# Sums of the experts' results in parts: quarters for one chunk behind the first mixture, halves for the last two chunks

## Chip, cores and metric

The kernel runs on one core of a Trainium2 chip. The metric is the device time of one execution in microseconds (us); a profile is one more execution of the same program.

## The reference

Two layers work on 4096 tokens of 256 numbers in float32, with a 4096 x 4096 adjacency matrix. Each layer is a graph step followed by a mixture of experts, both with a layer norm ahead and a residual around:

```
x = x + gnn0(layernorm(x), adj)          # graph step, then a state-space scan
x = x + moe0(layernorm(x))               # 8 experts, the best 2 for each token
x = x + gnn1(layernorm(x), adj, adj)     # tanh(adj*adj), 700 largest of each row kept
x = x + moe1(layernorm(x))               # 6 experts, the best 2 for each token
```

A mixture's output for a token is `w0 * y0 + w1 * y1`: the outputs of its two experts with the routing weights. In the second graph step the node features are `h = tanh(xn @ W_proj + b)`, then `g = h @ W_gcn`, and the result is `relu(A @ g + b)` with A the filtered adjacency matrix.

## The kernel before

Tokens go in chunks of CW = 512, of TPC = 4 tiles of 128 tokens; there are NC = 8 chunks. Token data lies with 128 tokens on the partitions.

**A mixture** first routes all tokens, then runs tiles of 256 gathered tokens (`expert_tiles`): SyncE (SP) loads the experts' weights `wk` and `bk`, POOL gathers the tokens `xk` with indirect DMAs, TensorE (PE) multiplies (`ps_xt`, `ps_h`, `ps_y`), and VectorE (DVE) adds the bias into `yk`. `put` (L391) then scatters `yk` by indirect DMA into a DRAM tensor `ys`, where every token has one row for its first and one for its second expert, arranged so that the four rows of a partition lie together: 4 KB for one partition of a chunk. The DMAs that scatter are kept in `dp.sent`.

**`combine`** fetches these rows again and sums. For each of the two experts it loads one tile `yg` (L516, 128 x 4 x 256, 512 KB; the pool has three such buffers) with an order behind the last four scatters, then makes eight `scalar_tensor_tensor` operations on VectorE (L524): for each of the four tiles of tokens, first `src + w0*yg0`, then `+ w1*yg1`. After the first mixture source and destination are both `x2`. After the second, the source is `x3`, the destination a tile `oc` that `to_out` stores to `out` (L1470).

**Between the first mixture and the second graph step**, `features_of` calls `combine` and then `node_features` for one chunk after each two pieces of the graph step's first column block: `layernorm` of the four tiles (statistics L76 and L77, the addition of eps L78 on VectorE, the power -0.5 on POOL L79, then `xn` on VectorE L81), TensorE transposes (L91, all four token tiles of column block 0, then all four of block 1), ACT copies them to `xnT` (L1359), TensorE makes `ps_lt` with `w_proj` (L140), ACT the tanh, TensorE `ps_gn` (L1367), ACT copies `gn`.

**The graph step** `propagate1(c)` goes through sixteen pieces of 256 rows of the transposed adjacency matrix: SP loads `at` (L1381, 512 KB, four buffers), VectorE makes `f = max(at, 0)` (L1387), ACT squares it and takes the tanh, VectorE counts the positive entries into `cnt` (L1392 for the first piece of a column block, L1394 for the others), and TensorE adds `gn x f` into `pf` (L1398). For column block 0, two pieces are done per chunk of features. So TensorE's order there is, for each chunk, transposes, `ps_lt`, `ps_gn`, then `pf` for two pieces.

**At the end**, the second mixture is in two dispatches: tokens of the first six chunks (`dp1[0]`), and of the last two (`dp1[1]`). The first six chunks' outputs are summed and stored while the second dispatch's tiles run. The last two chunks (`for b in range(NC - SPLIT)`) come when all its tiles are done. Behind the whole stands a test (`flag`) for a rarely needed second way, which begins with a full top-700 selection and then repeats the mixture; it is not taken with these inputs.

**What sets the order**: the middle of the program (the scan) has an order written out by hand. Around the change no order is written: a scheduler of the framework orders each engine's instructions when the program is built, and the engines then take them strictly in that order. SP issues its DMAs in order as well, so a DMA that waits for a buffer holds up those behind it.

Of the kernel before, what the change touches and what calls it, by code (L numbers as in the profile page):

```python
# [9 lines left out]
F32 = mybir.dt.float32  # L10
# [3 lines left out]
ALU = mybir.AluOpType  # L14
# [4 lines left out]
P = 128  # L19
CW = 512  # L20
TPC = CW // P
# [7 lines left out]
def kernel(ctx: ExitStack, tc: tile.TileContext, out: bass.AP, **a):  # L29
    nc = tc.nc  # L30
    x, adj, adjT = a["x"], a["adj"], a["adjT"]
    N, D = x.shape
# [12 lines left out]
    def tokens(ap, c):  # L45
        return ap[c * CW:(c + 1) * CW, :].rearrange("(t p) d -> p t d", p=P)
# [22 lines left out]
    def layernorm(src, dst):  # L69

        T = src.shape[1]
        st = small.tile([P, T, 6], F32, name="ln_st")
        mv = small.tile([P, T, 2], F32, name="ln_mv")
        rs = small.tile([P, T], F32, name="ln_rs")
        for t in range(T):
            nc.vector.bn_stats(st[:, t, :], src[:, t, :])  # L76
            nc.vector.bn_aggr(mv[:, t, :], st[:, t, :])  # L77
        nc.vector.tensor_scalar(rs, mv[:, :, 1], EPS, None, ALU.add)  # L78
        nc.gpsimd.tensor_tensor(rs, rs, mhalf[:, :T], ALU.pow)  # L79
        for t in range(T):  # L80
            nc.vector.tensor_scalar(  # L81
                dst[:, t, :], src[:, t, :], mv[:, t, 0:1], rs[:, t:t + 1],
                ALU.subtract, ALU.mult,
            )
# [60 lines left out]
    def after(later, earlier):  # L145
        tc.add_manual_dep(
            later.ins, earlier.ins.name,
            mybir.DependencyInfo(mybir.DependencyClass.Sync, mybir.DependencyReason.DATA),
            reason="order",
        )  # L150
# [355 lines left out]
                also(n)  # L506
        finish(*prev)

    def combine(dp, pool, c, src, dst):


        yg = []
        for i in range(2):
            yg.append(pool.tile([P, TPC, D], F32, name="yg", bufs=3))
            r0 = (i * dp.S + c) * CW
            ld = nc.sync.dma_start(  # L516
                yg[i], dp.ys[r0:r0 + CW, :].rearrange("(p t) d -> p t d", t=TPC)
            )
            for o in dp.sent[-4:]:
                after(ld, o)  # L520
        for t in range(TPC):
            s_ = c * TPC + t
            for i in range(2):
                nc.vector.scalar_tensor_tensor(  # L524
                    dst[:, t, :], yg[i][:, t, :], dp.wv[:, s_, i:i + 1], (src, dst)[i][:, t, :],
                    ALU.mult, ALU.add,
                )

    r0 = ctx.enter_context(tc.tile_pool(name="route0", bufs=1))
# [7 lines left out]
    with ExitStack() as s1:  # L539
# [44 lines left out]
        dp = Dispatch(r0, E0, "d0", [NT - 2 * TPC, 2 * TPC])  # L584
# [571 lines left out]
        with tc.manual_schedule(engines={  # L1156
# [11 lines left out]
            for _ in range(2 * NT + 2):  # L1168
                i = min(range(STEPS), key=lambda i: pe[i] - PE_RATIO * dve[i])
# [23 lines left out]
            for n in range(NC * STEPS):  # L1193
                c, i = divmod(n, STEPS)
# [24 lines left out]
                old, das = das, []  # L1219
# [52 lines left out]
    x2 = keep.tile([P, NT, D], F32, name="x2")  # L1272
    wp = ctx.enter_context(tc.tile_pool(name="w_ffn0", bufs=1, reuse_waits="tile"))
    with ExitStack() as s2:
        with ExitStack() as st:
# [47 lines left out]
        x3 = keep1.tile([P, NT, D], F32, name="x3")  # L1323
# [9 lines left out]
        dp1 = [  # L1333
            Dispatch(keep1, E1, "d1a", [TPC] * SPLIT),
            Dispatch(keep1, E1, "d1b", [TPC] * (NC - SPLIT), SPLIT),
        ]
# [15 lines left out]
        ps_f = s2.enter_context(tc.tile_pool(name="ps_f", bufs=2, space=PSUM, reuse_waits="tile"))  # L1352
        ps_m = s2.enter_context(tc.tile_pool(name="ps_m1", bufs=4, space=PSUM, reuse_waits="tile"))

        def node_features(c):
            xn = wk.tile([P, TPC, D], F32, name="xn", tag="xn_r")
            layernorm(x2[:, c * TPC:(c + 1) * TPC, :], xn)
            xT = wk.tile([P, DB, CW], F32, name="xnT2", tag="fm", bufs=4)
            transpose_chunk(ps_m, "m", xn, lambda k, ps: nc.scalar.copy(xT[:, k, :], ps))  # L1359
            h2 = wk.tile([P, DB, CW], F32, name="h2", tag="fm", bufs=4)  # L1360
            layer_T(ps_m, "m", xT, w_proj, AF.Tanh, b_proj, h2, DB, DB)
            for hh in range(TPC // 2):
                ps = ps_m.tile([P, 2, D], F32, name="ps_gn", tag="m")
                for j in range(2):
                    t = 2 * hh + j
                    for k in range(DB):
                        nc.tensor.matmul(  # L1367
                            ps[:, j, :], h2[:, k, t * P:(t + 1) * P], w_gcn[:, k, :],
                            start=(k == 0), stop=(k == DB - 1),
                        )  # L1370
                t0 = c * TPC + 2 * hh
                nc.scalar.copy(gn[:, t0:t0 + 2, :], ps)
# [47 lines left out]
        def features_of(j2):  # L1420

            if j2 % (TPC // 2) == 0:
                c = j2 // (TPC // 2)
                rows = x2[:, c * TPC:(c + 1) * TPC, :]
                combine(dp, wk, c, rows, rows)
                node_features(c)

        early = [route1(d, wk, ps_m, ("m", "m", "m"), 4) for d in dp1]

# [32 lines left out]

    stores = []

    def to_out(d, b, pool):

        c = d.c0 + b
        o = pool.tile([P, TPC, D], F32, name="oc")
        combine(d, pool, b, x3[:, c * TPC:(c + 1) * TPC, :], o)
        return nc.sync.dma_start(tokens(out, c), o)  # L1470


    few = [2 * d.NT * P // TR + E1 // 2 for d in dp1]
    with ExitStack() as s4:
        tp = s4.enter_context(tc.tile_pool(name="tiles1", bufs=2, reuse_waits="tile"))
        psums = [
            s4.enter_context(tc.tile_pool(name=n, bufs=f, space=PSUM, reuse_waits="tile"))
            for n, f in (("ps_h1", 3), ("ps_o1", 2), ("ps_t1", 2))
        ]
        ps_r = s4.enter_context(tc.tile_pool(name="ps_r1", bufs=1, space=PSUM, reuse_waits="tile"))  # L1480
        sr = ExitStack()
        rp = sr.enter_context(tc.tile_pool(name="route1", bufs=2, reuse_waits="tile"))
        late = route1(dp1[1], rp, ps_r, ("m", "m", "m"), 1)

        def routing():
            late.prepare(NC - 1 - SPLIT)
            yield
            late.choose(NC - 1 - SPLIT)
            yield
            yield from dp1[1].tables(  # L1490
                ps_r.tile([P, CW], F32, name="ps_inv", tag="m"), rp, [eb1, eb2]
            )

        pieces = routing()
        ready, op = list(range(SPLIT)), []

        def also(n):
            if n == few[0]:
                assert next(pieces, None) is None
                sr.close()  # L1500
                op.append(s4.enter_context(tc.tile_pool(name="out1", bufs=2, reuse_waits="tile")))
            elif n < few[0]:
                if n > 0:
                    next(pieces, None)
            elif (n - few[0]) % 3 != 0 and ready:
                stores.append(to_out(dp1[0], ready.pop(0), op[0]))

        tiles1([(d, k) for d, f in zip(dp1, few) for k in range(f)], psums, tp, also)
        assert not ready

        for b in range(NC - SPLIT):
            stores.append(to_out(dp1[1], b, op[0]))


        flag = small.tile([1, 1], F32, name="flag", bufs=1)
        flagi = small.tile([1, 1], I32, name="flagi", bufs=1)
        nc.vector.tensor_reduce(flag, cmax, AX.X, ALU.max)
        nc.vector.tensor_scalar(flag, flag, TOPK + 0.5, None, ALU.is_gt)
        for d, f in zip(dp1, few):
            nc.vector.scalar_tensor_tensor(flag, d.tiles, f + 0.5, flag, ALU.is_gt, ALU.add)  # L1520

        after(nc.vector.tensor_copy(flagi, flag), dp1[1].sent[-1])
        again = nc.values_load(flagi[0:1, 0:1], min_val=0, max_val=3)
# [3 lines left out]
    with tc.If(again > 0):  # L1527
# [57 lines left out]
        with ExitStack() as s3:  # L1585
            kp = s3.enter_context(tc.tile_pool(name="again", bufs=1))
            d = Dispatch(kp, E1, "d2", [TPC] * NC)
            d.lo = lo1
            with ExitStack() as sr:
                ps_r = sr.enter_context(tc.tile_pool(name="ps_r2", bufs=2, space=PSUM))  # L1590
                rp = sr.enter_context(tc.tile_pool(name="route2", bufs=1))
                rt = route1(d, rp, ps_r, ("m", "m", "m"), 1)
                for c in range(NC):
                    rt.prepare(c)
                    rt.choose(c)
                for _ in d.tables(ps_r.tile([P, CW], F32, name="ps_inv", tag="m"), rp, [eb1, eb2]):
                    pass
            psums = [
                s3.enter_context(tc.tile_pool(name=n, bufs=f, space=PSUM))
                for n, f in (("ps_h2", 3), ("ps_o2", 2), ("ps_t2", 2))  # L1600
            ]
            with tc.tile_pool(name="tiles2", bufs=2) as tp:
                tiles1([(d, k) for k in range(d.K)], psums, tp)
            op = s3.enter_context(tc.tile_pool(name="out2", bufs=1))
            for c in range(NC):
                after(to_out(d, c, op), stores[c])


# [65 lines left out]
```

## Time and profile before

| | |
|---|---|
| median of 3 runs | 2479.3 us (2477.19 to 2481.99) |
| the profiled execution's own time | 2478.58 us |
| its span, first to last instruction | 2476.7 us |
| mean granted TensorE clock | 0.956 of full speed |
| busy share of the span: PE, DVE, ACT, POOL | 91%, 67%, 48%, 46% |
| sums `x<-yg` behind the first mixture | 64, from 1633.2 to 1697.6 us |
| sums `oc<-yg` of the last two chunks | 16, from 2462.5 to 2469.7 us |
| loads `yg<-d_ys` of 512 KB | 16, median 4.4 us from issue to landing |

Times in the views are microseconds from the start of the span; a line of a timeline gives start, duration, engine, line of the kernel, operation and tiles, and in brackets the idle time of the engine before it with what ended it. SPq is SP's queue: it issues DMAs and the duration is that of the issue, not of the transfer. In the chain of waits each piece is the step that ended last, followed back from the end.

### The profile page before, as it was taken

What the parts mean: (1) busy time and instruction counts of PE and PEld (TensorE: products, weight loads), DVE (VectorE), ACT (ScalarE), POOL (GpSimd) and SP (SyncE); (2) the same over time, 40 slices, a digit from 0 to 9 for tenths busy, and PEclk for the clock granted to TensorE, in tenths of its full rate; (3) what the DMA queues carried; (4) which work ended last, traced back from release to release, by engine and by line L of the source; (5) the groups of instructions that cost most, each with busy time, mean ns of one, the idle gap of its engine ahead of it and who ended that gap; (6) DMA issues with size and microseconds to landing.
All of it is one profiled execution on the core that took longest, in us unless ns stands there. A gap on an engine that the chain in (4) does not pass through costs nothing. (4 is left out here: it accounts for less than half of the span.)

```text
span 2476.7 us, 25809 instructions
## 1 busy us (share of the span) xinstructions
PE 2259.5 (91%) x8024; PEld 1448.7 (58%) x8024; DVE 1652.7 (67%) x2368; ACT 1194.0 (48%) x2029; POOL 1141.4 (46%) x830
## 2 busy tenths in 40 slices
PE   5989989999999999896994999969999999989985
PEld 4765655646565565643663888845544444458874
DVE  4049999999999999989897111165466666744233
ACT  1135657465665657466662322224566566633321
POOL 1027677777767677776551455411000000026652
PEclk9989999999999999997996999989999999999998
DMA  6259898999999999988655777743344444447886
GB/s 205 94 161 240 229 269 225 268 220 269 238 244 266 234 264 231 274 239 216 214 175 172 232 232 233 216 162 108 102 145 146 144 146 149 139 133 235 245 279 233
DMA packets 290500, 509.33 MB, mean 206 GB/s; under 512 B 25376, under 2 KB 157600, under 8 KB 289456
## 3 DMA queue, kind: packets, MB, share of 16 engines
q1 hardware_dynamic: 244080, 410.55, 52.9%
q0 software_dynamic: 46272, 97.03, 18.3%
q8 instruction: 67, 1.10, 0.2%
q14 instruction: 81, 0.66, 0.1%
HBM read 406.03 MB, written 42.73 MB: 181 GB/s over the span
## 5 line engine op out<-in xcount | busy, mean ns | idle before, releaser
L1103 POOL TENSOR_TENSOR db<-du,bb 128x1024 f32<-128x1024 f32 x256 | 607.0, 2371 | 359.5 <-ACT state L1124 132.4
L1118 DVE TENSOR_TENSOR_SCAN db<-da,state,db 128x512 f32<-128x512 f32 x512 | 627.5, 1267 | 45.7 <-ACT da L1111 43.4
L642 PE MATMUL pt<-at,gn 128*128 128x256 f32 x2048 | 488.2, 391 | 33.9 <-DVE ln_mv L77 27.4
L1111 ACT ACTIVATE da<-dt,negA 128x512 f32<-128x512 f32 x512 | 347.5, 691 | 354.3 <-DVE db L1118 352.5
L642 PEld LDWEIGHTS pt<-at,gn 128*128 128x128 f32 x2048 | 398.3, 196 | 164.7 <-issue 74.6
L1398 PE MATMUL pf<-f,gn 128*128 128x512 f32 x1024 | 450.4, 594 | 0.0
L1145 PE MATMUL psy<-hc,ident 128*128 128x512 f32 x576 | 304.3, 622 | 46.5 <-DMA hc<-hc 40.1
L1128 DVE TENSOR_TENSOR hc<-db,cb 128x1024 f32<-128x1024 f32 x256 | 331.8, 1296 | 17.9
L1398 PEld LDWEIGHTS pf<-f,gn 128*128 128x128 f32 x1024 | 191.5, 190 | 224.9 <-issue 223.8
L79 POOL TENSOR_TENSOR ln_rs<-ln_rs,mhalf 128x4 f32<-128x4 f32 x24 | 34.5, 1436 | 513.4 <-DVE ln_rs L78 454.0
L460 DVE TENSOR_TENSOR yk<-ps_y,bk 128x512 f32<-128x512 f32 x73 | 50.5, 691 | 326.9 <-PE ps_y L455 302.4
L470 PE MATMUL ps_h<-xkT,wk 128*128 128x256 f32 x864 | 214.7, 390 | 12.5 <-DVE xkT L495 8.4
L1388 ACT ACTIVATE f<-f 128x1024 f32<-128x1024 f32 x128 | 135.3, 1057 | 180.6 <-DVE f L1387 178.8
L455 PE MATMUL ps_y<-wk,hk 128*128 128x256 f32 x864 | 210.9, 380 | 0.2
L1387 DVE TENSOR_SCALAR f<-at 128x1024 f32<-128x1024 f32 x128 | 88.2, 689 | 174.9 <-PE pf L1398 158.1
L1132 POOL DMA_DIRECT2D hc<-hc x224 | 195.0, 870 | 0.2
L470 PEld LDWEIGHTS ps_h<-xkT,wk 128*128 128x128 f32 x864 | 160.7, 194 | 47.1 <-ACT hk L474 11.2
L1145 PEld LDWEIGHTS psy<-hc,ident 128*128 128x128 f32 x576 | 110.5, 198 | 122.9 <-issue 51.2
L455 PEld LDWEIGHTS ps_y<-wk,hk 128*128 128x128 f32 x864 | 161.4, 190 | 21.8 <-ACT hk L474 1.3
L474 ACT ACTIVATE hk<-ps_h,d_b 128x256 f32<-128x256 f32 x140 | 66.2, 474 | 184.2 <-PE ps_h L470 184.2
L1394 DVE SCALAR_TENSOR_TENSOR cnt<-at,cnt 128x1024 bf16<-128x1024 f32 x120 | 146.1, 1217 | 11.6 <-DMA at<-in_adjT_dram 10.5
L754 PE MATMUL ps_xz<-hT,w_in 128*128 128x512 f32 x256 | 126.4, 630 | 14.7 <-ACT hT L742 14.7
(307 smaller groups left out, 2585.6 us busy)
## 6 DMA issues: line engine op xcount, KB each, us to landing
at<-in_adjT_dram SPq DMA_DIRECT2D x256, 512.0 KB, 4.3
bb<-bcd SPq DMA_DIRECT2D x128, 512.0 KB, 5.1
cb<-bcd SPq DMA_DIRECT2D x128, 512.0 KB, 4.7
hc<-hc POOLq DMA_DIRECT2D x224, 256.0 KB, 5.6
wk<-in_L_ffn_W_dram SPq DMA_DIRECT2D x70, 512.0 KB, 5.0
wk<-in_L_ffn_expert_w_dram SPq DMA_DIRECT2D x114, 256.0 KB, 4.4
yg<-d_ys SPq DMA_DIRECT2D x16, 512.0 KB, 4.4
yd<-us SPq DMA_DIRECT2D x6, 1024.0 KB, 7.9
```

Of the source, the lines that this page charges most:

```text
L455: nc.tensor.matmul(ps[:, j, :], hT[:, m, j * P:(j + 1) * P], w[:, m, :], start=(m == 0), stop=(m == kb_out - 1),)
L470: nc.tensor.matmul(ps[:, j, :], w[:, d, m * P:(m + 1) * P], xT[:, d, :], start=(d == 0), stop=(d == DB - 1),)
L642: nc.tensor.matmul(pt[:, k, :], xl[:, j, k * P:(k + 1) * P], at[:, jj, :], start=(j == 0 and k == 0), stop=(j == NT - 1 and k == DB - 1),)
L1103: nc.gpsimd.tensor_tensor(self.db, self.f.du[self.half][:, self.mi:self.mi + 1, :].to_broadcast([P, 2, CW]), self.bb, ALU.mult,)
L1111: nc.scalar.activation(da, self.f.dt[self.half][:, self.mi, :], AF.Exp, scale=negA[:, self.m, n:n + 1])
L1118: nc.vector.tensor_tensor_scan(self.db[:, j, :], da, self.db[:, j, :], state[:, self.m, n:n + 1], ALU.mult, ALU.add,)
L1128: nc.vector.tensor_tensor(self.hc, self.db, self.cb, ALU.mult)
L1132: nc.gpsimd.dma_start(self.hc[:, 0, :], self.hc[:, 1, :], accum_op=ALU.add)
L1145: nc.tensor.matmul(f.psy[m], ident, self.hc[:, j, :], start=False, stop=(self.g == GS - 1 and j == last),)
L1388: nc.scalar.activation(f, f, AF.Square)
L1394: nc.vector.scalar_tensor_tensor(cnt, at, 0.0, cnt, ALU.is_gt, ALU.add)
L1398: nc.tensor.matmul(pf[:, k, :], gn[:, j, k * P:(k + 1) * P], f[:, jj, :], start=(j == 0), stop=(j == NT - 1),)
```

## The change

`combine` gets a number of parts and becomes a generator: for each part it loads the two `yg` tiles of that part alone (128 x T x 256 with T = 4, 2 or 1), makes the part's sums, and yields. `node_features` now calls `combine` itself and normalises each part as it comes: four parts of 128 tokens for chunk 0, one part for the other seven. `to_out` stores each part by itself: two parts for the last two chunks, one for the first six. The number of `yg` buffers stays three. The loop of the second way at the bottom follows the new return value.

```diff
-    def combine(dp, pool, c, src, dst):
-        yg = []
-        for i in range(2):
-            yg.append(pool.tile([P, TPC, D], F32, name="yg", bufs=3))
-            r0 = (i * dp.S + c) * CW
-            ld = nc.sync.dma_start(
-                yg[i], dp.ys[r0:r0 + CW, :].rearrange("(p t) d -> p t d", t=TPC)
-            )
-            for o in dp.sent[-4:]:
-                after(ld, o)
-        for t in range(TPC):
-            s_ = c * TPC + t
+    def combine(dp, pool, c, src, dst, parts=1):
+        T = TPC // parts
+        for t0 in range(0, TPC, T):
+            yg = []
             for i in range(2):
-                nc.vector.scalar_tensor_tensor(
-                    dst[:, t, :], yg[i][:, t, :], dp.wv[:, s_, i:i + 1], (src, dst)[i][:, t, :],
-                    ALU.mult, ALU.add,
-                )
+                yg.append(pool.tile([P, T, D], F32, name="yg", tag="yg", bufs=3))
+                r0 = (i * dp.S + c) * CW
+                rows = dp.ys[r0:r0 + CW, :].rearrange("(p t) d -> p t d", t=TPC)
+                ld = nc.sync.dma_start(yg[i], rows[:, t0:t0 + T, :])
+                for o in dp.sent[-4:]:
+                    after(ld, o)
+            for t in range(T):
+                s_ = c * TPC + t0 + t
+                for i in range(2):
+                    nc.vector.scalar_tensor_tensor(
+                        dst[:, t0 + t, :], yg[i][:, t, :], dp.wv[:, s_, i:i + 1],
+                        (src, dst)[i][:, t0 + t, :], ALU.mult, ALU.add,
+                    )
+            yield
...
-        def node_features(c):
+        def node_features(c, parts):
+            rows = x2[:, c * TPC:(c + 1) * TPC, :]
             xn = wk.tile([P, TPC, D], F32, name="xn", tag="xn_r")
-            layernorm(x2[:, c * TPC:(c + 1) * TPC, :], xn)
+            T = TPC // parts
+            for i, _ in enumerate(combine(dp, wk, c, rows, rows, parts)):
+                layernorm(rows[:, i * T:(i + 1) * T, :], xn[:, i * T:(i + 1) * T, :])
...
                 c = j2 // (TPC // 2)
-                rows = x2[:, c * TPC:(c + 1) * TPC, :]
-                combine(dp, wk, c, rows, rows)
-                node_features(c)
+                node_features(c, TPC if c == 0 else 1)
...
-    def to_out(d, b, pool):
-        c = d.c0 + b
+    def to_out(d, b, pool, parts=1):
+        c, T = d.c0 + b, TPC // parts
         o = pool.tile([P, TPC, D], F32, name="oc")
-        combine(d, pool, b, x3[:, c * TPC:(c + 1) * TPC, :], o)
-        return nc.sync.dma_start(tokens(out, c), o)
+        sent = []
+        for i, _ in enumerate(combine(d, pool, b, x3[:, c * TPC:(c + 1) * TPC, :], o, parts)):
+            part = slice(i * T, (i + 1) * T)
+            sent.append(nc.sync.dma_start(tokens(out, c)[:, part, :], o[:, part, :]))
+        return sent
...
-            stores.append(to_out(dp1[1], b, op[0]))
+            stores.append(to_out(dp1[1], b, op[0], 2))
...
-                after(to_out(d, c, op), stores[c])
+                for new in to_out(d, c, op):
+                    for old in stores[c]:
+                        after(new, old)
```

## The prediction

> **What bounds the kernel now.** I read the page's line of busy times (PE 91% of the span), then the two places the change touches. The first is the passage from the first mixture to the graph layer. Windows (window: length, then per engine busy time and count, granted PE clock, DMA share, GB/s):
>
> ```profile
> 1621.20:1640.70 19.50, 0.00 (x0) 0.00 (x0) 12.04 (x33) 0.00 (x0) 3.40 (x7) 0.62 0.63 211
> 1640.70:1658.60 17.90, 17.82 (x48) 9.68 (x49) 16.10 (x49) 4.47 (x7) 3.08 (x2) 0.84 0.49 183
> 1658.60:1767.10 108.50, 105.77 (x339) 58.82 (x337) 50.56 (x127) 54.61 (x72) 8.05 (x5) 1.00 0.28 92
> ```
>
> TensorE stands still for 19.5 us, then works without a hole for eight chunks of about 15.3 us. So only what brings its restart at 1640.7 forward or back counts. The chain of waits and the timelines (start, length, what) show what it waits for:
>
> ```profile
> 1605.26 22.73 DMA d_ys<-yk,d_dst
> ...
> 1633.16 3.25 DVE x L524 x8
> ...
> 1638.94 1.22 POOL ln_rs L79
> 1640.18 1.38 DVE xn L81 x4
> ```
>
> ```profile
> 1628.16 1.28 SPq L516 DMA_DIRECT2D yg<-d_ys  x3
> 1628.78 0.69 DVE L1392 TENSOR_SCALAR cnt<-at 128x1024 bf16<-128x1024 f32 x1
> 1629.50 3.74 DVE L1394 SCALAR_TENSOR_TENSOR cnt<-at,cnt 128x1024 bf16<-128x1024 f32 x3
> 1633.16 3.25 DVE L524 SCALAR_TENSOR_TENSOR x<-yg,d_wv,x 128x256 f32<-128x256 f32 x8
> 1640.18 1.38 DVE L81 TENSOR_SCALAR xn<-x,ln_mv,ln_rs 128x256 f32<-128x256 f32 x4 [0.94 <-POOL ln_rs L79]
> 1640.74 2.10 PE L91 MATMUL ps_tr<-ident,xn 128*128 128x128 f32 x8 [19.56 <-DVE xn L81]
> ```
>
> The scattered results land, SP issues the loads at 1628.16, and they land at 1631.7 and 1633.0. VectorE meanwhile does four counts (`cnt`) until 1633.2: **the loads are hidden behind the counts**. From the first sum to the last `xn` (1641.56) are 8.40 us. The second place is the end, where the chain alternates between loads and sums:
>
> ```profile
> 2456.42 2.41 DMA d1b_ys<-yk,d1b_dst
> 2458.98 3.45 DMA yg<-d1b_ys
> 2462.46 1.68 DVE oc L524 x4
> 2464.16 4.25 DMA yg<-d1b_ys
> ```
>
> **The change at the first chunk.** Bytes and sums stay. Two loads of 512 KB become eight of 128 KB, one 128x4 power on POOL becomes four of 128x1, one `ln_rs` addition becomes four. The four counts still stand ahead of the first sum, so quicker first loads gain nothing: the first sum stays at 1633.16. What the diff does not tell is the order of VectorE's instructions in the built program. Three more counts, which in the kernel before come after chunk 1, now stand inside chunk 0:
>
> ```
> sum p0, sum p0, stats p0, sum p1, aggr p0, eps p0, xn p0 [waits POOL],
> CNT, sum p1, sum p2, stats p1, sum p2, aggr p1, stats p2, eps p1,
> CNT, xn p1 [POOL], aggr p2, CNT, eps p2, sum p3, xn p2 [POOL],
> sum p3, stats p3, sum chunk 1, aggr p3, sum chunk 1, eps p3, sum chunk 1, xn p3 [POOL]
> ```
>
> VectorE takes them in order, and transposes, ACT and TensorE stand in the same order as before. TensorE transposes column block 0 of all four parts before block 1, so it goes no further than p3 lets it.
>
> Paces from the timeline, start to start: independent sums 0.40, dependent ones 0.51 (0.48 and 0.03 wait), stats 0.33, aggregate or eps 0.08, `xn` 0.32, a count 1.14 (1.22 less overlap). The power of 128x1 does not occur. Nearest rows:
>
> ```profile
> 1306.75 0.70 POOL L1046 TENSOR_TENSOR x_dev<-x_dev,mhalf 128x2 f32<-128x2 f32 x1 [18.50 <-DVE x_dev L1045]
> 1646.06 1.17 POOL L79 TENSOR_TENSOR ln_rs<-ln_rs,mhalf 128x4 f32<-128x4 f32 x1 [5.92 <-DVE ln_rs L78]
> 1653.89 1.91 POOL L79 TENSOR_TENSOR ln_rs<-ln_rs,mhalf 128x4 f32<-128x4 f32 x1 [6.65 <-DVE ln_rs L78]
> ```
>
> From 128x2 to 128x4 is 0.47, so 128x1 may be 0.55 at best and 1.2 at worst; I take 0.85, nearer to the 128x2 row. The third row ran beside a count and took 0.7 more; of the new powers only p1's does, so it costs 0 to 0.7 (I take 0.35).
> - p0 to the issue of its `xn`: two dependent sums 1.03; stats, sum, aggregate, eps 1.08; POOL 0.97 with its two hand-overs; `xn` 0.32. Sum 3.40.
> - then up to the second count: count 1.14, sums and p1's and p2's statistics 2.04. Sum 3.18.
> - second count 1.14, `xn` 0.32, aggregate 0.09, third count 1.14, eps and hand-over 0.25. Sum 2.94.
> - p2's POOL and hand-over 0.89, `xn` 0.32, last sum 0.51, p3's statistics with two sums of chunk 1 1.45, POOL 0.88, last `xn` 0.41. Sum 4.46.
>
> 13.98 instead of 8.40: **+5.6, with p1's crowded power +5.9**. With powers of 0.55 and none crowded it is +4.7, with 1.2 and 0.7 crowded +7.4. Three counts (3.4) and the three extra trips to POOL make it up.
>
> *Loads.* Three `yg` buffers serve four parts, so a load waits for the sum that frees a buffer: p1's second load goes at 1633.7, p2's at 1634.2 and 1635.0, p3's at 1638.2 and 1638.6. A lone 128 KB load (`rw`) landed in 2.1, a 512 KB one in 3.1, so each is there 1 us or more before VectorE gets to it: cost 0. Behind a waiting load on SP's queue stand the `at` loads of the second and third inner count: issued at about 1635.4 and 1635.8, landed after 3.6 and 4.4 at 1639.0 and 1640.2, wanted at 1639.7 and 1641.3. Their cover is 0.7 and 1.1; the `at` loads of before landed after up to 7.5 behind 1 MB of `yg`. If that returns, p3 is up to 3 us later still. The Trainium skill (DMA: Bandwidth & Descriptors, section Bandwidth) speaks against the change in another way: it advises batching transfers to 1 MiB or more. By the fixed 2.0 us and rate of its section on the anatomy of one DMA (GpSimd path), an estimate for three rounds of 128 KB is 6.9 us, over by 1635; that alone would price this part at 0.
>
> *Clock.* The granted clock is 0.50 from 1640.7 to 1645.0; the longer idle stretch moves this slow start with the work, cost 0. The Trainium skill (TensorE: Matmul & The Clock Gate, Part 1) has the gate open after a busy free-running window of about 3.4 us; by that the slow start may differ by up to one window at half rate, 1.7 us either way.
>
> *What is late next.* Chunk 1's last `xn` ends at 1648.65 and TensorE takes it at 1658.60: 10 us of cover. With chunk 1 loaded and summed about 6.7 later and TensorE 5.9 later, 9 remain, and later chunks have more (VectorE needs about 11.5 us a chunk: eight sums 3.2, statistics and eps 2.1, wait for POOL 0.9, `xn` 1.4, two counts 2.4, two `f` 1.4; TensorE 15.3). So TensorE's whole row moves by 5.9, and all behind it is released by TensorE or what follows from it.
>
> **The change at the end.** Two 512 KB loads and one 512 KB store a chunk become four and two of 256 KB; sums and bytes stay. A lone 256 KB load (`wk`) landed in 2.53. First half at 2461.5 instead of 2462.4; but the fourth load waits for a buffer, and SP's order puts each store ahead of later loads. Fourth load 2462.5 to 2465.05; two sums and the store's issue to 2466.4; load of the last half, behind that store's data, 2.8 to 2469.2; its partner, freed at 2467.5, at 2470.05; two sums 0.88; last store at 2471.0 instead of 2470.2: +0.8. It carries half the bytes: 256 KB stores (`d_xd` from `at`) landed in 2.1 where this one took 3.18: -0.6 to -1.1. I take 0, and -0.8 to +1.5 as ends (a store in the way, or one round less).
>
> **The sum.** The profiled execution took 2478.58 (span 2476.7 and 1.9 around it), 0.7 below the median 2479.3 of the three runs. 2478.58+5.9+0 = 2484.5 on its own time, 2485.2 by the median; as every leftover (several semaphores on one wait) adds, I say 2485.5.
>
> **Rivals.**
> - *Slower as worked out*: 0.68. Its own range is +3.9 (4.7-0.8) to +8.9 (7.4+1.5): 2483.2 to 2488.2.
> - *The inner counts wait for data too*, because the `at` loads land as late as they did before: +5.9 and up to 3, so +7 to +9, about 2487.5. For it: 7.36, 6.64 and 7.50 us in this very stretch. Against: 1 MB less is ahead of them. 0.10.
> - *The shift is absorbed*: of 450 us from 1767 to 2217 TensorE is idle 10.4, and if fixed moments set that, the delay would sink in: -0.8 to +1.5, about 2479.6. Against: those waits end on VectorE and POOL steps that follow TensorE's own results. 0.12.
> - *Faster: parts flow*. If the inner counts lay in VectorE's waits, p3's loads would be the limit: landed near 1637, then sum 0.48, stats 0.41, aggregate and eps 0.32, POOL 0.97, `xn` 0.41 give 1639.6, 2.0 earlier; with 0.8 at the end -2.8, 2476.5, and up to -5.5 with a clock window won (1.7) and 1.0 more at the end. The point of decision is whether all three counts come after p3; the built order says no. 0.10.
>
> **Numbers.** 0.2% is 5.0 us, about what a measurement of this kernel can tell from no change. Slower by more holds most of the first case and all of the second: 0.68. The rest of the first and the absorbed case are within: 0.23. The last case and a little luck of the clock: 0.09. The range from 2480.0 to 2489.0 leaves out the fast case and most of the absorbed one.
>
> **What would show it.** Right: the first sum still near 1633; three counts between it and the last `xn`; four powers of 0.6 to 1.2; the transposes' idle time near 25 rather than 19.56 (it splits, as the first part's transposes come early); chunk spacing on TensorE unchanged at 15.3; the last store issued within 1 us of 2470.2 plus the shift. Wrong: counts behind p3, PE's first `ps_lt` before 1645, or a last `xn` later than 1650.

## The result, and the profile after

The changed kernel took 2488.15 us (median of 16 runs, 2478.42 to 2493.49), the kernel before 2478.24 (16 runs beside it, 2472.45 to 2486.21). The ratio is 1.0037, 95% interval 1.0025 to 1.0049: 9.2 us slower, 6.2 to 12.1 (the two medians lie 9.9 apart). The profiled execution took 2489.03 us, its span 2487.2. Single executions of one kernel lie some 14 us apart, so where the time went is read from marks inside the two profiles:

| us from the start of the span | before | after | shift |
|---|---|---|---|
| first load of `yg` behind the first mixture | 1628.16 | 1628.25 | +0.1 |
| first sum | 1633.16 | 1633.24 | +0.1 |
| last `xn` of chunk 0 ends | 1641.56 | 1647.14 | +5.6 |
| first `ps_lt` | 1642.87 | 1648.35 | +5.5 |
| first `pf` | 1651.74 | 1658.16 | +6.4 |
| end of column block 0 (first product with `cnt`) | 1767.55 | 1774.99 | +7.4 |
| second mixture's first tile | 2204.08 | 2212.53 | +8.5 |
| first load of `yg` at the end | 2458.98 | 2466.27 | +7.3 |
| last store issued | 2470.20 | 2481.49 | +11.3 |
| end of the span | 2476.73 | 2487.25 | +10.5 |

Two steps stand out: 5.5 us at the first chunk, and 3.2 us in the last twenty. What lies between adds 1.8 and moves both ways.

**The first chunk.** The windows of after (length; busy time and count of PE, PEld, DVE, ACT and POOL; granted PE clock, DMA share, GB/s):

```profile
1621.20:1647.20 26.00, 2.06 (x8) 0.87 (x7) 17.25 (x42) 0.00 (x0) 5.60 (x10) 0.60 0.59 190
1647.20:1665.03 17.83, 17.37 (x43) 8.85 (x44) 14.84 (x47) 5.73 (x8) 2.13 (x2) 0.82 0.47 156
1665.03:1774.50 109.47, 105.81 (x339) 58.81 (x337) 47.60 (x123) 53.34 (x70) 6.93 (x5) 1.00 0.28 88
```

The window up to TensorE's last transposes has grown from 19.50 to 26.00; the two behind it have kept their length within 1 us. Its timeline shows that the parts do reach it one by one, but only as transposes of 0.7 us that nothing can follow:

```profile
1636.62 0.66 PE L91 MATMUL ps_tr<-ident,xn 128*128 128x128 f32 x2 [15.39 <-DVE xn L81]
1641.68 0.69 PE L91 MATMUL ps_tr<-ident,xn 128*128 128x128 f32 x2 [4.41 <-DVE xn L81]
1644.19 0.69 PE L91 MATMUL ps_tr<-ident,xn 128*128 128x128 f32 x2 [1.82 <-DVE xn L81]
1647.20 0.69 PE L91 MATMUL ps_tr<-ident,xn 128*128 128x128 f32 x2 [2.32 <-DVE xn L81]
1648.35 6.34 PE L140 MATMUL ps_lt<-xnT,w_proj 128*128 128x512 f32 x8 [0.46 <-ACT xnT L1366]
```

The idle time in the brackets is 15.39+4.41+1.82+2.32 = 23.9 us; before it was 19.56. `ps_lt` needs all four tiles, so only the last pair sets the restart. VectorE's timeline in that stretch:

```profile
1633.24 1.00 DVE L525 SCALAR_TENSOR_TENSOR x<-yg,d_wv,x 128x256 f32<-128x256 f32 x2
...
1636.06 0.41 DVE L81 TENSOR_SCALAR xn<-x,ln_mv,ln_rs 128x256 f32<-128x256 f32 x1 [0.70 <-POOL ln_rs L79]
1636.39 1.22 DVE L1401 SCALAR_TENSOR_TENSOR cnt<-at,cnt 128x1024 bf16<-128x1024 f32 x1
...
1639.55 1.22 DVE L1401 SCALAR_TENSOR_TENSOR cnt<-at,cnt 128x1024 bf16<-128x1024 f32 x1
1641.21 0.41 DVE L81 TENSOR_SCALAR xn<-x,ln_mv,ln_rs 128x256 f32<-128x256 f32 x1 [0.45 <-POOL ln_rs L79]
...
1641.63 1.19 DVE L1401 SCALAR_TENSOR_TENSOR cnt<-at,cnt 128x1024 bf16<-128x1024 f32 x1
...
1646.73 0.41 DVE L81 TENSOR_SCALAR xn<-x,ln_mv,ln_rs 128x256 f32<-128x256 f32 x1 [0.44 <-POOL ln_rs L79]
```

The three counts stand between the parts, and the idle time of VectorE that the brackets show is four waits for POOL, 0.70, 0.45, 0.44 (at 1643.72) and 0.44, 2.0 us together. POOL's four powers:

```profile
1635.45 0.58 POOL L79 TENSOR_TENSOR ln_rs<-ln_rs,mhalf 128x1 f32<-128x1 f32 x1 [6.76 <-DVE ln_rs L78]
1639.72 1.46 POOL L79 TENSOR_TENSOR ln_rs<-ln_rs,mhalf 128x1 f32<-128x1 f32 x1 [3.69 <-DVE ln_rs L78]
1642.97 0.71 POOL L79 TENSOR_TENSOR ln_rs<-ln_rs,mhalf 128x1 f32<-128x1 f32 x1 [1.79 <-DVE ln_rs L78]
1646.04 0.65 POOL L79 TENSOR_TENSOR ln_rs<-ln_rs,mhalf 128x1 f32<-128x1 f32 x1 [2.36 <-DVE ln_rs L78]
```

**The end.** The chain of waits of after (start, length, what):

```profile
2466.65 4.45 DMA yg<-d1b_ys
...
2471.20 1.29 DVE oc L525 x3
...
2472.59 4.09 DMA yg<-d1b_ys
...
2476.77 0.89 DVE oc L525 x2
2477.68 2.81 DMA yg<-d1b_ys
```

Two rounds of loads on the chain have become three, and two of the three last over 4 us. From the first load to the last store are now 15.22 us instead of 11.22; the smaller last store gives 0.8 back (5.76 from its issue to the end of the span instead of 6.53), which leaves +3.2.

### The profile page after: what moved, and what is told of

Its sections match the earlier page's. It is cut to its first block, busy times and chain, and to the rows that moved or that the text cites. A ratio compares the mean times of both kernels' runs of the same rounds, so it can differ in the third digit from the quotient of the medians.

```text
span 2487.2 us, 25838 instructions
## 1 busy us (share of the span) xinstructions
PE 2269.2 (91%) x8024; PEld 1454.7 (58%) x8024; DVE 1653.1 (66%) x2371; ACT 1194.2 (48%) x2029; POOL 1141.5 (46%) x833
## 5 line engine op out<-in xcount | busy, mean ns | idle before, releaser
L644 PE MATMUL pt<-at,gn 128*128 128x256 f32 x2048 | 493.7, 394 | 32.7 <-DVE ln_st L76 27.4
L79 POOL TENSOR_TENSOR ln_rs<-ln_rs,mhalf 128x4 f32<-128x4 f32 (+1 forms) x27 | 34.6, 1281 | 521.7 <-DVE ln_rs L78 521.7
L470 PE MATMUL ps_h<-xkT,wk 128*128 128x256 f32 x864 | 216.3, 393 | 11.3 <-DVE xkT L495 8.6
L1395 ACT ACTIVATE f<-f 128x1024 f32<-128x1024 f32 x128 | 135.3, 1057 | 181.6 <-DVE f L1394 179.8
L1401 DVE SCALAR_TENSOR_TENSOR cnt<-at,cnt 128x1024 bf16<-128x1024 f32 x120 | 146.0, 1217 | 16.9 <-DMA at<-in_adjT_dram 16.2
L1396 ACT ACTIVATE f<-f 128x1024 f32<-128x1024 f32 x128 | 135.2, 1056 | 3.8
```

Of the source, the lines that this page charges most:

```text
L470: nc.tensor.matmul(ps[:, j, :], w[:, d, m * P:(m + 1) * P], xT[:, d, :], start=(d == 0), stop=(d == DB - 1),)
L644: nc.tensor.matmul(pt[:, k, :], xl[:, j, k * P:(k + 1) * P], at[:, jj, :], start=(j == 0 and k == 0), stop=(j == NT - 1 and k == DB - 1),)
L1395: nc.scalar.activation(f, f, AF.Square)
L1401: nc.vector.scalar_tensor_tensor(cnt, at, 0.0, cnt, ALU.is_gt, ALU.add)
```

## The experiments

**Theory A**: the first chunk loses by what stands in VectorE's order, three counts and three extra trips to POOL; the tail loses by rounds of loads (a round is a load that can start only when earlier sums have freed a buffer), since three small buffers make more of them. **Rival C** for the first chunk: the quarter loads come late (in the last of these runs, as Theory C, by their small buffers). **Rival B**: for the tail, loads and stores of 256 KB slow each other (in one run as Theory B); for the whole, the tail only echoes the later start. **Rival D**: trips to POOL are dear by themselves. The twelve kernels ran in three groups of four; each group shares one chip and its runs of the kernel before (medians 2493.5, 2498.8 and 2478.1). The second mixture took 268 to 273 us from its first tile to the tail on the first two chips and 255 to 259 on the third, so only ratios within a group and lengths of stages are compared. The intervals of the ratios are 3 to 5 us to either side; the stages carry the verdicts. Each stage is read from one profile; how steady that is, unchanged stages show: from the first sum to the last `xn` 8.40 us in before, e2, e4 and e6, from the first load to the end of column block 0 139.38 to 139.40; a tail in one part took 11.16 to 11.49 us to the last store and 17.66 to 18.03 to the end of the span in eight profiles. The edits are shown shortened; `...` stands for lines left out.

**1. The first chunk alone and the tail alone.** Each undoes one call:

```diff
-            stores.append(to_out(dp1[1], b, op[0], 2))
+            stores.append(to_out(dp1[1], b, op[0], 1))      # e1_front_only
...
-                node_features(c, TPC if c == 0 else 1)
+                node_features(c, 1)                         # e2_tail_only
```

> The quarters of the first chunk alone; the last two chunks go in one part, as before. Theory A (the two edits cost separately and add up): the last xn of the first chunk ends near 1647.1, column block 0 ends near 1775.0 (7.4 later than before), and the end is as before: about 11.2 us from the first load of the tail to the last store, 17.75 to the end of the span. Time near 2478.2+7 = 2485. Rival B (the whole loss is made by the first chunk, and the tail's longer way is an echo of the later start): tail 21 us again and about 2488.

> The halves of the last two chunks alone; the first chunk goes in one part, as before. Theory A: first chunk as before (last xn near 1641.6, column block 0 ends near 1767.5), the tail takes about 15.2 us from the first load to the last store and 21.0 to the end, so the time is 3.2 above before, near 2481.5. By my prediction's sum the tail would cost 0 (2478.2).

| | before | after | first chunk alone | tail alone |
|---|---|---|---|---|
| first sum to last `xn` | 8.40 | 13.90 | 13.91 | 8.40 |
| first load to end of column block 0 | 139.39 | 146.74 | 145.46 | 139.40 |
| tail: first load to last store | 11.22 | 15.22 | 11.43 | 15.44 |
| tail: first load to end of span | 17.75 | 20.98 | 17.96 | 21.17 |
| ratio to before, interval | | 1.0037, 1.0025 to 1.0049 | 1.0024, 1.0005 to 1.0043 | 1.0005, 0.9987 to 1.0023 |

The edits are independent: each stage is slow where its own edit is in, and as before elsewhere. First chunk +6.1, tail +3.4 from these two profiles. The echo is out. The whole time of the tail alone can't show its 3.4 within its interval.

**2. What holds up the first chunk.** Four kernels, all with the tail in one part, take the counts, the trips and the rounds of loads away in turn. The counts are ordered behind chunk 0's last `xn`; the layer norm goes once over the chunk; or the quarters are loaded into slices of whole tiles, so that no load waits for a buffer:

```diff
+                if c == 0 and 4 <= j2 < 8:                  # e3, e9, e10: counts behind
+                    after(count, normed[0])
...
-                layernorm(rows[:, i * T:(i + 1) * T, :], xn[:, i * T:(i + 1) * T, :])
+                pass                                        # e5, e9, e10: one norm
+            layernorm(rows, xn)
...
+        all_ = [pool.tile([P, TPC, D], F32, name="yg", tag="yg", bufs=bufs) for _ in range(2)]
         for t0 in range(0, TPC, T):                         # e10, e11: no rounds
-            yg = []
+            yg = [y[:, t0:t0 + T, :] for y in all_]
```

> The quarters of the first chunk alone, and the counts of pieces 5 to 8 of column block 0 are ordered behind the last xn of the first chunk; nothing else of the work changes. Theory A (the three counts in VectorE's order are 3.4 us of the 5.5, and what p1's power loses beside a count is 0.7 more): last xn 9.8 to 10.5 us after the first sum instead of 13.90, that is 1643.0 to 1643.8, column block 0 ends 3 to 4 us earlier than with the quarters alone, time near 2481.5. Rival C (the quarter loads are what holds the parts up; the counts only fill VectorE's waits): last xn stays within 1 us of 13.90.

> The quarters of the first chunk for loads and sums alone; the layer norm goes once over the whole chunk (one power of 128x4 instead of four of 128x1), with the counts where the scheduler puts them. Theory A (the extra trips to POOL are the rest, about 2 us): eight sums 3.3, counts 2.3 to 3.4, statistics, power and four xn 5.2 give 10.8 to 11.9 us from the first sum to the last xn. Rival C (quarter loads late): about 13.9. Time near 2482.5 by A.

> Quarters of the first chunk for loads and sums, one layer norm over the whole chunk, and the counts of pieces 5 to 8 behind its last xn; the tail in one part. The first chunk then has neither the inner counts nor the three extra trips to POOL, only the quarter loads with three buffers. Theory A (counts 3.4 us, POOL trips the rest, about 2): last xn 8.4 to 9.2 us after the first sum. Rival C (quarter loads in several rounds hold it up): 10 us or more, as in the run with the norms in parts and the counts behind (10.53). Time near that of the kernel before.

> As the run with one norm and the counts behind (10.94 us from the first sum to the last xn), but the quarter loads go into slices of whole yg tiles, so that none waits for a buffer. The first four counts stay ahead of the sums. If the rounds of loads are what was left (VectorE waited 0.92, 0.47 and 0.60 for quarter loads there): 8.4 to 9.1 us. If something else is left, such as the small loads landing late by themselves: 10 or more. The tail goes in one part.

> The change's first chunk in all (quarters, four norms, no order given to the counts), with one difference: the quarter loads go into slices of whole yg tiles and wait for no buffer. In the built order the scheduler now puts the inner counts behind the last xn by itself. Theory C (three small buffers cause both losses: the rounds of loads, and by them the counts ahead of the later parts): 9 to 10.2 us from the first sum to the last xn instead of 13.90, of which what exceeds the run with one norm is the price of the four trips to POOL (0.5 to 1.5). Theory A (POOL trips 2 us or more): 10.5 or more. The tail goes in one part.

| kernel | counts inside | loads in rounds | norms | first sum to last `xn` | first load to end of column block 0 | ratio, interval |
|---|---|---|---|---|---|---|
| before | no | no (512 KB) | 1 | 8.40 | 139.39 | |
| e1 (the change here) | 3 | yes | 4 | 13.91 | 145.46 | 1.0024, 1.0005 to 1.0043 |
| e5 | 3 | yes | 1 | 13.76 | 144.79 | 1.0028, 1.0010 to 1.0046 |
| e3 | 0 | yes | 4 | 10.53 | 141.42 | 1.0002, 0.9988 to 1.0017 |
| e9 | 0 | yes | 1 | 10.94 | 142.39 | 0.9998, 0.9982 to 1.0015 |
| e11 | 0 | no | 4 | 10.30 | 140.62 | 1.0004, 0.9990 to 1.0018 |
| e10 | 0 | no | 1 | 8.50 | 139.88 | 1.0011, 1.0000 to 1.0023 |

*The counts* are worth 13.91-10.53 = 3.4 us of the last `xn` and 4.0 us at the end of the column block, as Theory A said (10.53 lies just above its 9.8 to 10.5). *The rest* is 2.1 us, and here Theory A held only in part. Taking away the trips to POOL gained nothing where loads came in rounds: e5 missed its 10.8 to 11.9 and e9 its 8.4 to 9.2. VectorE's timeline of e9 shows what took the place of POOL:

```profile
1636.18 0.48 DVE L526 SCALAR_TENSOR_TENSOR x<-yg,d_wv,x 128x256 f32<-128x256 f32 x1 [0.92 <-DMA yg<-d_ys]
...
1638.08 0.48 DVE L526 SCALAR_TENSOR_TENSOR x<-yg,d_wv,x 128x256 f32<-128x256 f32 x1 [0.47 <-DMA yg<-d_ys]
...
1639.84 1.00 DVE L526 SCALAR_TENSOR_TENSOR x<-yg,d_wv,x 128x256 f32<-128x256 f32 x2 [0.60 <-DMA yg<-d_ys]
```

Three waits for quarter loads, 2.0 us. With loads that wait for no buffer and one norm (e10), 8.50 is left, nearly that of before: Rival C's loads are late by their buffers, not by their size, as long as four counts stand ahead of the sums. With four norms and no rounds (e11) VectorE waits for POOL instead, four times in a row:

```profile
1636.48 0.41 DVE L81 TENSOR_SCALAR xn<-x,ln_mv,ln_rs 128x256 f32<-128x256 f32 x1 [0.47 <-POOL ln_rs L79]
...
1638.81 0.41 DVE L81 TENSOR_SCALAR xn<-x,ln_mv,ln_rs 128x256 f32<-128x256 f32 x1 [0.34 <-POOL ln_rs L79]
...
1640.58 0.41 DVE L81 TENSOR_SCALAR xn<-x,ln_mv,ln_rs 128x256 f32<-128x256 f32 x1 [0.44 <-POOL ln_rs L79]
...
1643.07 0.41 DVE L81 TENSOR_SCALAR xn<-x,ln_mv,ln_rs 128x256 f32<-128x256 f32 x1 [0.44 <-POOL ln_rs L79]
```

So trips alone cost 10.30-8.50 = 1.8, rounds alone 10.94-8.50 = 2.4, both together 10.53-8.50 = 2.0: they lie beside each other, and removing one uncovers the other. e11's 10.30 lies between Theory C's 9 to 10.2 and Theory A's 10.5 or more, and its trips cost more than the 0.5 to 1.5 expected.

e11 tells one thing more. It is given no order for the counts, and yet the scheduler puts them behind the last `xn` once the quarter loads need no buffer. So the small buffers also brought the counts in.

In e5 a further rival of the prediction appeared, that the inner counts wait for their own data:

```profile
1643.38 1.22 DVE L1402 SCALAR_TENSOR_TENSOR cnt<-at,cnt 128x1024 bf16<-128x1024 f32 x1 [0.57 <-DMA at<-in_adjT_dram]
...
1644.96 1.23 DVE L1402 SCALAR_TENSOR_TENSOR cnt<-at,cnt 128x1024 bf16<-128x1024 f32 x1 [0.26 <-DMA at<-in_adjT_dram]
```

Their loads were issued behind waiting `yg` loads. In the changed kernel itself the counts did not wait.

**3. Parts that flow, with all eight counts behind.** The first four counts are moved as well (`0 <= j2 < 8` in the edit above), so that sums start with the first quarter. e7 has one norm and its tail is that of e4 below; e8 has four norms and the tail in one part.

> Candidate. First chunk in quarters for loads and sums, loaded into slices of whole tiles so that no part waits for a buffer, one layer norm over the chunk, and the counts of pieces 1 to 8 all behind its last xn; the tail as in the run without buffer waits. If rounds and counts are what the change loses by: last xn 10 to 11 us after the first load (before 13.4, with the change 18.9), so about 2.5 less than before; time 2 to 4 us below before.

> Candidate. As the last one, but with the layer norm part by part as in the change, and the tail in one part. Theory A (a trip to POOL costs little when the next part's sums lie in it and no count does): last xn 8.5 to 10 us after the first load, 3.5 to 5 less than before. Rival D (the four trips to POOL are dear by themselves, 2 us in all): later than in the run with one norm, 11 to 12.5.

| | first load to first sum | to last `xn` | to first `pf` | to end of column block 0 | ratio, interval |
|---|---|---|---|---|---|
| before | 5.00 | 13.40 | 23.58 | 139.39 | |
| e7 | 2.31 | 11.72 | 22.42 | 139.04 | 1.0005, 0.9988 to 1.0022 |
| e8 | 2.54 | 13.08 | 22.78 | 141.33 | 0.9991, 0.9978 to 1.0004 |

The first sum came 2.5 to 2.7 earlier, the last `xn` 1.7 and 0.3. Both missed their ranges (10 to 11 and 8.5 to 10). Behind the first sum VectorE waited for quarter loads, 0.49 and 0.36 us in e7 and 0.65 in e8, though none of these loads waits for a buffer; in e10 the four counts covered that. e8 also waited three times for POOL, 0.34, 0.44 and 0.44, and is later than e7 and than Rival D's 12.5. And little of the gain reached the end of the column block. e8 gave back 2.74 us after the first `pf`. TensorE waited there for `xnT` at two later chunks, 0.65 and 1.98 us, where before it waited 0.88 and 0.89, so 0.9 more; and behind the longer wait its clock was halved once more, as the windows of e8 show (the third number from the end is the granted clock):

```profile
1685.00:1691.70 6.70, 4.74 (x18) 2.30 (x16) 6.70 (x17) 2.62 (x4) 2.45 (x1) 1.00 0.59 204
1691.70:1697.20 5.50, 5.48 (x10) 2.43 (x11) 5.50 (x18) 3.20 (x5) 0.20 (x1) 0.69 0.65 217
1697.20:1705.00 7.80, 7.80 (x27) 4.76 (x26) 6.08 (x18) 1.82 (x3) 2.66 (x2) 1.00 0.01 3
```

The eight `ps_lt` of that chunk took 5.40 us instead of 3.70, another 1.7.

**4. The tail.** Halves alone, first with slices of whole tiles (as above; with 4 as the number of `yg` tiles no load waits for a buffer), then with small buffers but one store a chunk, and last with slices and the stores issued by ACT's queue (in a kernel with the first chunk of e7):

```diff
-        for i, _ in enumerate(combine(d, pool, b, x3[:, c * TPC:(c + 1) * TPC, :], o, parts)):
+        for i, _ in enumerate(combine(d, pool, b, x3[:, c * TPC:(c + 1) * TPC, :], o, parts,
+                                      4 if isinstance(op, list) and pool in op else 3)):   # e4, e12
...
-            sent.append(nc.sync.dma_start(tokens(out, c)[:, part, :], o[:, part, :]))
+            if i == parts - 1:                                                     # e6
+                sent.append(nc.sync.dma_start(tokens(out, c), o))
...
-            sent.append(nc.sync.dma_start(tokens(out, c)[:, part, :], o[:, part, :]))
+            sent.append((nc.scalar if parts > 1 else nc.sync).dma_start(            # e12
+                tokens(out, c)[:, part, :], o[:, part, :]))
```

> Halves of the last two chunks alone, but each half is loaded into its half of a whole yg tile and the pool out1 has four of these, so that no load of the tail waits for a buffer; two of the eight loads still stand behind a store on SP's queue. Theory A (the tail loses by rounds: three small buffers make four rounds of loads, each with its fixed time): last store 10 to 12 us after the first load of the tail, against 15.2 with three buffers and 11.2 before. Rival B (loads and stores of 256 KB under way at the same time slow each other, whatever the buffers): 14 us or more.

> Halves of the last two chunks for loads and sums alone, with three small buffers, but one store of 512 KB for each chunk: on SP's queue six loads, a store, two loads, a store. Theory A (the tail loses by rounds of loads): last store 13.5 to 14.7 us after the first load, end 19.5 to 21. Theory B (stores between and beside the loads): last store 11.5 to 12.8, end near 18.

> Candidate. First chunk as in the run with slices, one norm and all eight counts behind (last xn 11.7 us after the first load); tail in halves with slices of whole tiles, and its four stores issued by ACT's queue, so that SP issues all eight loads without waiting for a sum or a store. If a load behind a store was the rest of the tail's loss (12.98 against 11.22 us): last store 10.3 to 11.3 after the first load, end 16.2 to 17.3 against 17.75 before. If loads and stores slow each other in the transfer itself: 12 to 13 again. Time 0 to 2 us below before.

| | first load to last store | to end of span | ratio, interval |
|---|---|---|---|
| before | 11.22 | 17.75 | |
| halves, three small buffers (e2) | 15.44 | 21.17 | 1.0005, 0.9987 to 1.0023 |
| the same, one store a chunk (e6) | 13.89 | 20.40 | 1.0021, 1.0009 to 1.0034 |
| no wait for a buffer (e4) | 12.98 | 18.70 | 1.0004, 0.9989 to 1.0018 |
| the same, stores by ACT (e12) | 10.84 | 16.06 | 0.9996, 0.9984 to 1.0008 |

The condition in the first edit gives four `yg` tiles to all sums of the first way's outputs, and it stands in e7, e8, e10 and e11 too. Buffers are worth 2.5 us at the end of the span (21.17 to 18.70), the stores' place on SP's queue 2.6 (18.70 to 16.06), 2.1 of it up to the last store. e7, which differs from e12 in the queue of the stores alone, took 12.87 and 18.60. A fourth buffer by itself is worth nothing: e8, e10 and e11, with four whole tiles and the tail in one part, took 11.16 to 11.27 to the last store and 17.66 to 17.77 to the end, as before. e4 came out above its 10 to 12, because the seventh and eighth load wait on SP until the sums ahead of the stores are done. e6, inside Theory A's 13.5 to 14.7, shows the same from the other side; its chain of waits has three rounds, and again the load behind a store is the long one:

```profile
2461.30 2.76 DMA yg<-d1b_ys
...
2464.99 2.97 DMA yg<-d1b_ys
...
2468.96 0.39 SPq L1477
...
2469.44 4.03 DMA yg<-d1b_ys
```

With both taken away, VectorE no longer waits once the second load has landed (timeline of e12):

```profile
2459.77 0.88 DVE L526 SCALAR_TENSOR_TENSOR oc<-yg,d1b_wv,x 128x256 f32<-128x256 f32 x2 [3.04 <-DMA yg<-d1b_ys]
2461.89 0.88 DVE L526 SCALAR_TENSOR_TENSOR oc<-yg,d1b_wv,oc 128x256 f32<-128x256 f32 x2 [1.24 <-DMA yg<-d1b_ys]
2462.68 0.88 DVE L526 SCALAR_TENSOR_TENSOR oc<-yg,d1b_wv,x 128x256 f32<-128x256 f32 x2
...
2466.64 0.88 DVE L526 SCALAR_TENSOR_TENSOR oc<-yg,d1b_wv,oc 128x256 f32<-128x256 f32 x2
```

e12's last store comes 0.4 us earlier in the tail than in the kernel before, the end of the span 1.7 (just below the 16.2 to 17.3 expected), and the end of column block 0 0.2. So most of the 1.7 lies behind the issue of the last store, 5.22 us to the end instead of 6.53; 0.8 of it comes with a store of half the size, as in e4 (5.71), and what the rest is stays open. Its median is 2476.94 against 2478.09: a gain of that size lies inside its interval, so it isn't shown to beat the kernel before.

## Why the prediction was right, and where it was not

The forecast was 2485.5 against a median of 2479.3, +6.2, with a range of 2480.0 to 2489.0; measured were 2488.15 and +9.2 on its own comparison. The direction held, and so did the price of the first chunk. The size was short by 3 us: 2488.15 lies inside the range, but at the very top of what "slower as worked out" allowed (2483.2 to 2488.2). In the two profiles the shift is 10.5 where the sum had 5.9: the first chunk gave 0.4 less, the way from there to the end of column block 0 1.9 more, and the tail, priced at 0, 3.2 more.

- *First sum unmoved*: held, 4.99 us after the first load instead of 5.00.
- *First chunk, 13.98 us to the last `xn`, +5.6, or the +5.9 with p1's crowded power that the sum took*: 13.90, +5.5. The counts were priced at 3.4 and measured at 3.4. The three trips to POOL were named as the rest, about 2; the sum is right, the reason only half. Rounds of loads lie beside the trips with the same length, so "cost 0" for the loads holds only as long as counts and trips cover them; e9 priced that cover at 2.4 us.
- *Powers of 128x1*: 0.58 to 0.71 where 0.85 was taken, and 1.46 beside a count where 0.85+0.35 was; together 3.40 against 3.75.
- *The order of the transposes was misread*: in the changed kernel they go in pairs, both column blocks of a part, not block 0 of all parts first. The idle time splits as said, and the end of it was the last part either way.
- *Clock, 0 within 1.7*: from the first `ps_lt` to the first `pf` are 9.81 us instead of 8.87, so +0.9. The windows of after show the half clock up to 1653.6, that is through 5.3 us of `ps_lt`; before it ended at 1646.3, after 3.4 (the prediction followed it to 1645.0 only):

```profile
1648.30:1653.60 5.30, 5.25 (x6) 2.19 (x7) 4.78 (x17) 1.17 (x2) 0.77 (x1) 0.50 0.61 205
1653.60:1658.20 4.60, 4.60 (x20) 3.42 (x19) 4.21 (x13) 1.27 (x2) 0.35 (x1) 0.99 0.14 25
```

Over the fourteen profiles the stretch took between 8.11 and 9.81, and the clock rose between 1.9 (e12) and 5.3 us (after) behind the first `ps_lt`, a spread of 3.4. The Trainium skill (TensorE: Matmul & The Clock Gate, Part 1) has the gate open after a busy window of about 3.4 us, from which the prediction's 1.7 came. The spreads of 1.7 and 3.4 agree with it, and so does e8 above, whose clock of 0.69 over 5.5 us is half rate for 3.4 us. Which way a kernel falls could not be known beforehand.
- *Only the restart counts, and later chunks have cover*: too simple, and here the mechanism was wrong. Before, `ps_lt` waited for `xnT` at chunk 1 and at chunk 2:

```profile
1660.52 3.70 PE L140 MATMUL ps_lt<-xnT,w_proj 128*128 128x512 f32 x8 [0.88 <-ACT xnT L1359]
1676.49 3.70 PE L140 MATMUL ps_lt<-xnT,w_proj 128*128 128x512 f32 x8 [0.89 <-ACT xnT L1359]
```

In all fourteen profiles the last such wait of more than 0.3 us sets the end of column block 0, which comes a fixed time behind it: 91.06 us behind chunk 2's (before, e2, e4, e6, e10), 75.74 or 75.75 behind chunk 3's (the others, but 77.44 in e8, with its clock halved there). A small difference in TensorE's restart is swallowed by this wait: in before, e2, e4 and e6, whose first chunk is the same, the slow clock put the first `pf` 22.90 to 23.58 us behind the first load, and the column block ended at 139.38 to 139.40 in all four. So +0.9 by the clock is no addend of its own in after, whose wait at chunk 3 was longer. VectorE's total leaves room for the later chunks, its order does not. In after, chunk 3 lost 2.38 us. The trace of waits reads backwards from TensorE to ACT to VectorE to a load:

```profile
1699.24 3.70 PE L140 MATMUL ps_lt<-xnT,w_proj 128*128 128x512 f32 x8 [2.38 <-ACT xnT L1366]
```

```profile
1696.57 1.06 ACT L1395 ACTIVATE f<-f 128x1024 f32<-128x1024 f32 x1 [6.83 <-DVE f L1394]
1697.66 1.06 ACT L1396 ACTIVATE f<-f 128x1024 f32<-128x1024 f32 x1
1698.62 1.05 ACT L1366 COPY xnT<-ps_tr 128x512 f32<-128x512 f32 x2
```

```profile
1688.71 1.23 DVE L1401 SCALAR_TENSOR_TENSOR cnt<-at,cnt 128x1024 bf16<-128x1024 f32 x1 [1.98 <-DMA at<-in_adjT_dram]
...
1695.85 0.69 DVE L1394 TENSOR_SCALAR f<-at 128x1024 f32<-128x1024 f32 x1
```

ACT's copies of `xnT` stand behind two operations on `f`, these behind VectorE's `f`, and VectorE had stood still 1.98 us for `at`. This `ps_lt` starts 71.0 us behind the first load, before chunk 3's started at 63.65: that is the +7.4 at the end of the column block where the sum had 5.9. In e1, with the same code there, VectorE waited 0.90 for `at` instead of 1.98, and the block ended 1.3 earlier. From the first `pf` to the end of the column block the profiles range from 114.7 (e11) to 118.6 (e8), against 115.8 before. The wait at chunk 3 is also what took back the gains of e7 (2.00 us) and e8 (1.98). There VectorE did not stand still; in the first window of e8 above it was busy all 6.70 us, and two counts stood ahead of `f`. That the counts moved back are what filled it is likely, but no run shows it alone.
- *Tail, 0 with -0.8 to +1.5*: this is the step that failed most, with +3.2. The queue order was right (fourth load waits for a buffer, stores ahead of later loads). The mis-sized term is the landing of a 256 KB load, for which the row of a lone load, 2.53, and 2.8 behind a store were used. The first landed after 2.85, but the second and third, in company, after 4.45 and 4.66, and the three issued behind and between the stores after 4.09, 3.88 and 4.32. So the partner of the last half, expected to be freed 8.5 us after the first load, was freed after 11.4. The Trainium skill (DMA: Bandwidth & Descriptors, section Bandwidth) advises batching transfers to 1 MiB or more; the runs agree for the change as built (+3.2 with 256 KB instead of 512), but with the same 256 KB loads e12 has its last store 0.4 us and its end 1.7 us earlier than before, so buffers and queue order decided here, not the size.
- *Rivals*: the shift was not absorbed behind column block 0 (the second mixture's first tile starts 584.3 us behind the first load in after and 583.5 in e1, against 575.9 before). "Parts flow" failed in the change for the reason given, and e7 and e8 show that even with all counts behind it would have been worth 0.35 us (e7) or less than nothing (e8, 1.9 later) at the end of the column block, not 2.

## What to carry to other kernels

In this tail a load cut into parts paid only when the parts also had their own buffers and nothing that waits was ahead of them on the queue; with as many small buffers as there were large ones, each part starts a new round, and here that cost 2.5 us in a tail of 18. Before letting one engine finish its work in parts, look at what the built order puts between the parts and at who can use a part: here three counts of 1.2 us came in, and the consumer needed all parts. Moving a restart is not yet moving the end: here a later wait, set by the order on VectorE and ACT, took back most of what the earlier restarts of e7, e8 and e12 had gained. A wait that is removed on an engine that works in order was only worth what the next one left (trips to POOL 1.8 us, rounds of loads 2.4, both 2.0), so price pairs of suspects together.

## What was not expected of the hardware

- In a row of loads the second lands late. In e12 loads of 256 KB issued 0.4 to 0.5 us apart landed at 2459.67, 2461.80, 2462.47, 2463.16 and 2463.78: 2.1 us from the first to the second, and 0.6 to 0.7 for each one behind. In after it were 2.0 us, before, with 512 KB, 2.6. So half the bytes brought the first load only 0.6 us forward (2.85 instead of 3.45).
- A pause of TensorE of about 2 us halved its clock in one kernel (e8, 1.98 us) and not in others (after 2.38, e10 2.14, e7 2.00, e12 1.99). What tells them apart is open. The Trainium skill (TensorE: Matmul & The Clock Gate, Part 1) names an idle window of about 3.4 us as what brings the slow clock back; here 1.98 us did once, so the measurement is below the rule, and it decides.
- The sixth of six or eight loads of 256 KB issued back to back took 1.50 us (e4), 1.17 (e7) and 1.95 (e12) on SP's queue, where the other issues took 0.33 to 0.43. Eight loads of 128 KB in a row (e7, e8) and four of 512 KB (e10, e11) showed nothing of the kind. Why is open.
- A power of 128x1 on POOL took 0.54 to 0.74 us, about the 0.70 of the one row of 128x2, and 1.46 while VectorE counted (after, e1).
